# A graph-attention and expert layer: first pair of graphs on raw x and raw W with rank-one corrections

## The chip, the cores and the metric

One core of one Trainium2 chip. The metric is device time in microseconds (us): the median of three runs, lower is better. A profile of one further execution shows what each engine did: PE (TensorE; its weight loads are listed apart as PEld), DVE (VectorE), ACT (ScalarE), POOL (GpSimd) and SP (which issues most transfers).

## The reference

x holds 128 graphs of 128 nodes with 1024 features each; adj holds one 0/1 matrix per graph. Cut to what matters:

```python
xn = layernorm(x)                               # mean and variance over the 1024 features
Wh = xn @ W                                     # W: 1024 x 1024, 16 heads of 64 columns
e = leaky_relu(Wh @ a1 + Wh @ a2, 0.2)          # one score per node and head
att = softmax(where(adj == 0, NEG_INF, e)) * adj
x = x + elu(att @ Wh)
xn = layernorm(x)
gates = softmax of the 2 largest of xn[:, 0] @ router.T, per graph
x = x + xn + sum over 8 experts of gates * (xn @ down.T) @ up
```

A score depends on its node alone, so a row of `att` is one number wherever adj is 1.

## The kernel before, in words

**Pairs.** The kernel works on pairs of graphs, q = 0 to 63. For each pair, `project(q)` multiplies a 256 x 1024 block of x with W by Winograd's variant of Strassen's scheme: seven products instead of eight, each of a 128 x 512 block with a 512 x 512 block. W's quarters are B11, B21, B22 and (in the slot of T1) W12; from them `combine` (L756) makes T3 = B22 - W12, T2 = T3 + B11, T1 = B22 - T2, NT4 = B21 - T2. On the side of x, `pair_sums` (L339 to L342, POOL) makes s1 to s4 from the transposed tiles `xt`. A product is 8 program matmuls in f32 (L383; 16 entries in the profile). Products 1 and 2 share the PSUM bank x, 6, 5 and 3 the bank y, 7 and 4 the bank z; there are two such PSUM buffers. `read` (L391, DVE) takes sums out of them: u2 after product 6, u4 after product 5, and the three blocks of `wh` later. Product 5 accumulates in the bank from which u2 is read.

**Layernorm without normalizing x.** W is centred (the mean of each column over the rows is taken off), so that x needs no mean subtraction, and 1/std (`RSTD`) is applied afterwards in `high` (L452, ACT) and `low` (L456, DVE), which split a result into two parts for the f32r matmuls of `attend` (L498). Scores come with the products: each block of W has four more columns, the centred W times a (260 columns instead of 256).

**The first pair.** All this has to be prepared while pair 0 is running; its centring of W is only done by `center_block` (L212, DVE) step by step. In the kernel before, pair 0 takes centred x (`center_x`, L186 to L196: means by PE, subtraction by DVE) times partly raw W; `correct_p1` (L771) mends p1, which the other products use. Column means of W come from `partial_means` (`fourths`, L180: four column tiles of PE of 32 columns at once), an ACT copy (L183) and `column_means` (L203). The score columns come from the transposed W: `score_rows` (L223), `center_rows` (L232 to L238), `turn_rows` (PE transposes, L247) and `score_columns` (L257 to L262, DVE). They are not ready for pair 0 itself: `score_of` multiplies pair 0's results with a (L273, POOL) and sums by head (L207, DVE).

**Order.** Nothing is scheduled by itself: every engine executes in the order in which the program records the instructions. `for q` (L804) fills eight lists, gaps[0] to gaps[7]; the tasks of gaps[i] are recorded just before the i-th product of the pair. `prepare` (L777) fills those of pair 0. Attention of pair q is done under the products of pair q + 1: `attention_weights` (L460) is in gaps[0] of pair q + 1, `attend` and `update` in gaps[1] and gaps[2], where `update` ends with L516 and L517 on DVE around an Exp on ACT (L515). Statistics of x are bn_stats and bn_aggr on DVE (`stats`, L312). The experts' tables (router, down) are centred once, during pair 1: `over_chunks` (L276) and `experts` (L286). A group of two pairs goes through the experts two pairs later.

**Transfers.** SP issues the loads in program order (from L117); adj_f goes through POOL's queue (L108). All x tiles, the transposed W's second half and, after the change, two more tiles share ten buffers with the tag "x".

## Time and profile before

| what | us |
| --- | --- |
| median of 3 runs | 1971.35 (1970.18 to 1971.63) |
| the profiled execution | 1970.7 |
| its span in the profile | 1968.8 |
| first product of pair 0 starts | 11.88 |
| score rows on PE (L223) start | 39.03 |
| first attention weights (L489, pair 0) | 69.45 |
| first product of pair 2 starts | 96.66 |

The span is the stretch in which the profile saw instructions; the execution's own time is 1.9 us longer. A line of the profile names the source line, the engine, the operation, the tile written and those read, with their shape. A wait is put down to whatever ended last before it, by semaphores. Idle time of an engine that is not the bottleneck costs nothing.

### The profile page before, as it was taken

To read this page: it belongs to the slowest core of one execution; us is meant where nothing else is said; L and a number is where in the kernel's file an instruction comes from. 1 tells how busy PE (TensorE), PEld (TensorE's weight loads), DVE (VectorE), ACT (ScalarE), POOL (GpSimd) and SP (SyncE) were. 2 spreads that over 40 slices of the span, in tenths; PEclk is the share of its full clock that TensorE was granted. 3 is DMA by queue.
4 is the path that set the end of the run, shared out by engine and by line. 5 is a ranking of instruction groups with operands and counts; after the bars stand their busy time and mean duration, and the time that the engine had idled before them with its cause. 6 is when DMAs were issued, how large, how long until landed. Compare 5 with 4: busy or idle time off the path is not lost.

```text
span 1968.8 us, 30168 instructions
## 1 busy us (share of the span) xinstructions
PE 1937.1 (98%) x11042; PEld 1575.5 (80%) x11042; DVE 1654.9 (84%) x3511; ACT 1080.4 (55%) x1032; POOL 833.1 (42%) x1123
## 2 busy tenths in 40 slices
PE   7899999999999999999999999999999999999997
PEld 4688888888888888888888888888888888888885
DVE  5888888888888888888898888898888898888886
ACT  1355555555655655555655655655655655655653
POOL 1443344543334543434544335544435544435530
PEclk9999999999999999999999999999999999999998
DMA  7265566565565565666565566565565565565552
GB/s 280 75 172 174 155 185 182 134 188 170 154 187 184 127 195 168 154 186 179 129 203 167 152 185 177 133 201 170 149 187 173 139 197 172 151 187 163 149 161 96
DMA packets 343671, 329.26 MB, mean 167 GB/s; under 512 B 274274, under 2 KB 276322, under 8 KB 342884
## 3 DMA queue, kind: packets, MB, share of 16 engines
q1 hardware_dynamic: 325940, 285.37, 49.6%
q0 software_dynamic: 17008, 40.91, 7.3%
q8 instruction: 88, 1.44, 0.3%
q10 hardware_dynamic: 576, 1.05, 0.1%
q14 instruction: 59, 0.48, 0.1%
HBM read 193.58 MB, written 67.63 MB: 133 GB/s over the span
## 4 chain that ended last, share of the span: by engine, by line
PE 91%; DVE 5%; DMA 2%; ACT 1%; issue 0%; POOL 0%; SPq 0%; DVEq 0%; POOLq 0%; ACTq 0%
PE pw L383 76%; PE ph L498 6%; PE pu L687 3%; PE pd L671 3%; DMA tt<-halves 1%; PE pb L634 1%; PE pl L578 1%; DVE stats L316 1%; DMA w_sb<-in_w 1%; ACT y_t L554 1%; DVE xn L516 1%; DVE hp L508 1%; DVE xn L517 1%; ACT halves L548 0%; PE pu L748 0%
## 5 line engine op out<-in xcount | busy, mean ns | idle before, releaser
L383 PE MATMUL pw<-w_sb,xt 128*128 128x260 f32 (+1 forms) x4096 | 953.0, 387 | 5.6 <-DVE parts L456 4.8
L383 PEld LDWEIGHTS pw<-w_sb,xt 128*128 128x128 f32 x4096 | 771.9, 191 | 153.5 <-issue 25.0
L383 PE MATMUL pw<-w_sb,s 128*128 128x260 f32 (+1 forms) x3072 | 712.9, 385 | 4.8 <-DVE w_sb L756 3.7
L383 PEld LDWEIGHTS pw<-w_sb,s 128*128 128x128 f32 x3072 | 579.6, 190 | 118.8 <-issue 24.8
L320 POOL TENSOR_SCALAR rstd<-mv 128x2 f32<-128x2 f32 x128 | 28.1, 219 | 868.0 <-DVE mv L317 862.7
L554 ACT COPY y_t<-tt 128x2048 uint16<-128x2048 uint16 x126 | 312.9, 2506 | 68.3 <-DMA tt<-halves 68.2
L316 DVE BATCH_NORM_STATS2 stats<-xn 128x6 f32<-128x512 f32 x512 | 323.8, 674 | 0.1
L652 POOL DMA_INDIRECT down<-table,at_down x248 | 251.4, 1014 | 163.8 <-DVE e L472 90.1
L548 ACT COPY halves<-xn 128x2048 uint16<-128x2048 uint16 x126 | 239.3, 1899 | 140.5 <-DVE xn L517 140.5
L452 ACT ACTIVATE parts<-wh,rstd 128x512 fp32r<-128x512 f32 x192 | 134.3, 716 | 224.0 <-DVE wh L391 223.8
L515 ACT ACTIVATE ex<-hp 128x1024 f32<-128x1024 f32 x128 | 135.3, 1057 | 182.6 <-DVE hp L508 182.6
L691 DVE SCALAR_TENSOR_TENSOR xn<-pu,rstd,xn 128x512 f32<-128x512 f32 x248 | 169.0, 744 | 21.8 <-PE pu L687 21.8
L508 DVE TENSOR_TENSOR hp<-ph,att 128x512 f32<-128x512 f32 x256 | 161.3, 671 | 10.0 <-PE ph L498 9.7
L498 PE MATMUL ph<-parts,adj_f 128*128 128x512 f32 x512 | 164.9, 442 | 4.5 <-DVE parts L456 3.7
L517 DVE SCALAR_TENSOR_TENSOR xn<-ex,xn 128x1024 f32<-128x1024 f32 x128 | 156.8, 1225 | 13.3
L391 DVE TENSOR_TENSOR wh<-pw,u 128x520 f32<-128x520 f32 (+1 forms) x128 | 89.2, 697 | 88.9 <-PE pw L383 85.5
L516 DVE SCALAR_TENSOR_TENSOR xn<-hp,xn 128x1024 f32<-128x1024 f32 x128 | 156.8, 1225 | 4.4
L570 ACT ACTIVATE xn<-xn,off,mul 128x1024 f32<-128x1024 f32 x128 | 151.4, 1233 | 1.5 <-POOL off L535 1.5
L456 DVE SCALAR_TENSOR_TENSOR parts<-wh,rstd,parts 128x512 fp32r<-128x512 f32 x192 | 139.4, 753 | 9.6 <-ACT parts L452 9.6
L498 PEld LDWEIGHTS ph<-parts,adj_f 128*128 128x128 f32 x512 | 96.5, 189 | 24.2 <-DVE parts L456 5.0
L391 DVE TENSOR_TENSOR wh<-pw,p 128x520 f32<-128x520 f32 (+1 forms) x64 | 44.7, 699 | 80.5 <-PE pw L383 80.5
L321 POOL TENSOR_TENSOR rstd<-rstd,half_pow 128x2 f32<-128x2 f32 x128 | 91.3, 713 | 10.7
(140 smaller groups left out, 1467.8 us busy)
## 6 DMA issues: line engine op xcount, KB each, us to landing
xt<-in_x_t SPq DMA_DIRECT2D x128, 512.0 KB, 5.2
xn<-in_x SPq DMA_DIRECT2D x128, 512.0 KB, 6.7
out_y<-xn SPq DMA_DIRECT2D x124, 512.0 KB, 3.8
adj_f<-in_adj_t POOLq DMA_DIRECT2D x32, 256.0 KB
adj_i<-in_adj SPq DMA_DIRECT2D x32, 256.0 KB, 2.6
w_sb<-in_w SPq DMA_DIRECT2D x4, 1040.0 KB, 7.3
down<-table,at_down POOLq DMA_INDIRECT x248, 3.7
wt_sb<-in_w_t SPq DMA_DIRECT2D x1, 2048.0 KB
```

Source lines behind the costliest of these rows:

```text
L316: nc.vector.bn_stats(st[:, h, :], X[i][:, h * HALF:(h + 1) * HALF])
L383: nc.tensor.matmul(dst[:, j, cols], lhs[:, k, :], w_sb[:, rhs, k, j, cols], start=(first and k == 0), stop=(k == KH - 1), skip_group_check ...
L456: nc.vector.scalar_tensor_tensor(in_two(PARTS[q][:, 1, b]), block, rstd, in_two(PARTS[q][:, 0, b].bitcast(F32)), op0=ALU.mult, op1=ALU.sub ...
L498: nc.tensor.matmul(PH[i][h], GRP[g]["adj_f"][:, t, :], PARTS[q][:, s, NH * (i % 2) + h], start=(s == 0), stop=(s == 1))
L508: nc.vector.tensor_tensor(hp[:, h * HALF:(h + 1) * HALF].rearrange("p (h f) -> p h f", f=F), ph.rearrange("p (h f) -> p h f", f=F), att[:, ...
L516: nc.vector.scalar_tensor_tensor(xt, hp, 0.0, xt, op0=ALU.max, op1=ALU.add)
L517: nc.vector.scalar_tensor_tensor(xt, ex, 1.0, xt, op0=ALU.min, op1=ALU.add)
L548: nc.scalar.copy(halves, X[i].bitcast(U16).rearrange("p (d s) -> p s d", s=2))
L554: nc.scalar.copy(y_of(i).bitcast(U16).rearrange("p k (n s) -> p s k n", s=2), TT.pop(i).rearrange("p (s k) n -> p s k n", s=2))
L570: nc.scalar.activation(X[i], X[i], AF.Identity, bias=GRP[g]["off"][:, t:t + 1], scale=GRP[g]["mul"][:, t:t + 1])
L652: nc.gpsimd.indirect_dma_start(out=st["down"][:, j * R:(j + 1) * R].rearrange("p r k -> p (r k)"), out_offset=None, in_=table, in_offset=b ...
L691: nc.vector.scalar_tensor_tensor(y[:, cols], pu[t], st["rstd"][:, t:t + 1], y[:, cols], op0=ALU.mult, op1=ALU.add)
```

## The change

In pair 0 x is no longer centred. Products 1 and 2 use raw x and raw B11 and B21, and `correct` (DVE, new L804) puts right their sum (c11, kept in SBUF) and p1 by adding the column means of W times minus the row sums of x; other products take centred or difference blocks, for which raw x is right. The transfers are put in another order and split. Twelve matmuls on a constant tile, whose result nobody reads, stand before the first product. The statistics of graphs 0 to 3 move from DVE to ACT, with small POOL steps (`sums_of`, `less`, `squares_of`). Pair 0's scores come from a PE product of xt with the score columns in column tiles (`first_scores`, in the middle of product 4, and `turn_scores`); score columns are placed by ACT (new L238) and combined by POOL (new L251 to L257). Sums over the experts' tables move from DVE to PE (`table_parts`). s3 of pair 0 gets its own tile, and within a product of pair 0 the two halves of the columns alternate. Line numbers of the kernel before hold elsewhere with a shift.

```diff
@@ -112,38 +111,48 @@
...
-    a_sum = work.tile([P, NH, 2, QC], F32, tag="ex", name="a_sum", bufs=1)
-    a_rows = work.tile([2, D], F32, tag="parts", name="a_rows", bufs=1)
-    nc.sync.dma_start(a_rows, a)
     a_cols = small.tile([P, 2, KC], F32, tag="a_cols", name="a_cols", bufs=1)
-    nc.sync.dma_start(a_cols, a_t)
-    load_xt(0)
+    nc.scalar.dma_start(a_cols, a_t)
+    xt = XT[0] = work.tile([P, 2, KC, P], F32, tag="xt", name="xt")
+    nc.sync.dma_start(xt[:, 0, 0:KH], x_t[0, :, 0:KH])
+    for k in range(0, KH, 2):
+        nc.sync.dma_start(w_sb[:, B11, k:k + 2], w[:, 0, k:k + 2])
+    nc.sync.dma_start(w_sb[:, B21], w[:, 1])
+    nc.sync.dma_start(xt[:, 0, KH:KC], x_t[0, :, KH:KC])
+    nc.sync.dma_start(xt[:, 1], x_t[1])
+    for i, b in ((2, B22), (3, T1)):
+        nc.sync.dma_start(w_sb[:, b], w[:, i])
+    load_x(0)
     wt_sb = work.tile([P, KH, D], F32, tag="y_t", name="wt_sb", bufs=1)
     wt_at = [wt_sb[:, c] for c in range(KH)]
     wt_at += [work.tile([P, D], F32, tag="x", name="wt", bufs=10) for _ in range(KH)]
-    for i, b in enumerate((B11, B21, B22, T1)):
-        if i == 2:
-            load_x(0)
-        nc.sync.dma_start(w_sb[:, b], w[:, i])
     nc.sync.dma_start(wt_sb, w_t[:, 0:KH])
     for c in range(KH, KC):
         nc.sync.dma_start(wt_at[c], w_t[:, c])
+    first_s3 = work.tile([P, 2, KH, P], F32, tag="x", name="first_s3", bufs=10)[:, 0]
+    scratch = work.tile([P, D], F32, tag="x", name="scratch", bufs=10)
     router_sb = const.tile([P, KC, E], F32, name="router_sb")
     down_sb = work.tile([P, G * TOP, R, KC], F32, tag="down", name="down_sb", bufs=1)
-    load_adj(0)
...
+    mean_of, sum_of = (work.tile([P, P], F32, tag="dn", name=n) for n in ("mean_of", "sum_of"))
+    nc.vector.memset(mean_of, 1.0 / D)
+    nc.vector.memset(sum_of, 1.0 / 32)
+    idle = ps_m.tile([P, P], F32, tag="pm", name="idle")
+    for _ in range(12):
+        nc.tensor.matmul(idle, mean_of, mean_of, start=True, stop=True)
...
-    mean_of, sum_of = (work.tile([P, P], F32, tag="dn", name=n) for n in ("mean_of", "sum_of"))
-    nc.vector.memset(mean_of, 1.0 / D)
-    nc.vector.memset(sum_of, 1.0 / 32)
+    fold = small.tile([P, H], F32, tag="fold", name="fold", bufs=1)
+    nc.vector.tensor_reduce(fold, ident.rearrange("p (t h) -> p h t", t=KH)[:, 0:H], AX.X, ALU.add)
@@ -163,37 +172,21 @@
...
-    def spread_a():
...
+    def fourths(*parts):
+        sizes = [rows[0].free_size() for rows in parts]
+        pc = ps_m.tile([P, HALF], F32, tag="pm", name="pc")[:, 0:sum(sizes)]
+        at = 0
+        for rows, n in zip(parts, sizes):
+            for u in range(2):
+                for c in range(KH):
+                    nc.tensor.matmul(pc[c * 32:(c + 1) * 32, at:at + n], mean_of[:, 0:32],
+                                     rows[u * KH + c], start=(u == 0), stop=(u == 1),
+                                     tile_position=(0, c * 32))
+            at += n
+        part = work.tile([P, HALF], F32, tag="hp", name="part")[:, 0:at]
...
-    def center_x():
@@ -240,54 +230,62 @@
...
+            for half in range(2):
+                nc.scalar.copy(
+                    a_two[:, u * KH:(u + 1) * KH, half * HPH:(half + 1) * HPH].rearrange(
+                        "p k (t f) -> p k t f", f=2),
+                    pt.rearrange("p k (t r) -> p k t r", t=KH)[:, :, :, 2 * half:2 * half + 2])
+    def score_columns():
+        def own(u, h):
+            return a_two[:, u * KH:(u + 1) * KH, h * HPH:(h + 1) * HPH].rearrange(
+                "p k (j c) -> p k j c", j=2)
         of = {b: w_sb[:, b, :, :, SCORES] for b in range(7)}
-        for h, u, dst in ((0, 0, of[B11]), (0, 1, of[B21]), (1, 1, of[B22]), (1, 0, b12)):
...
-    def score_of(b):
...
-    def over_chunks():
...
+        b11, b21, b22, b12 = own(0, 0), own(1, 0), own(1, 1), own(0, 1)
+        nc.gpsimd.tensor_copy(of[B11], b11)
+        nc.gpsimd.tensor_tensor(of[T3], b22, b12, ALU.subtract)
+        nc.gpsimd.tensor_tensor(of[T2], of[T3], b11, ALU.add)
+        nc.gpsimd.tensor_copy(of[B21], b21)
+        nc.gpsimd.tensor_tensor(of[T1], b22, of[T2], ALU.subtract)
+        nc.gpsimd.tensor_copy(of[B22], b22)
+        nc.gpsimd.tensor_tensor(of[NT4], b21, of[T2], ALU.subtract)
+    def first_scores():
+        ps = ps_m.tile([P, HALF], F32, tag="pm", name="ps")[:, 0:2 * P]
+        for u in range(2):
+            for c in range(KH):
+                k = u * KH + c
+                nc.tensor.matmul(ps[c * 32:(c + 1) * 32], a_two[:, k], xt[:, :, k],
+                                 start=(u == 0), stop=(u == 1), tile_position=(0, c * 32))
+        part = work.tile([P, 2, P], F32, tag="hp", name="part")
+        nc.scalar.copy(part, ps.rearrange("p (t n) -> p t n", t=2))
+        return part
+    def turn_scores(part):
+        ps = ps_m.tile([P, HALF], F32, tag="pm", name="ps")
+        for t in range(2):
+            nc.tensor.matmul(ps[:, t * H:(t + 1) * H], part[:, t], fold, start=True, stop=True)
+        SC[0] = small.tile([P, 2, H], F32, tag="sc0", name="sc0", bufs=1)
+        nc.scalar.copy(SC[0], ps[:, 0:2 * H].rearrange("p (t h) -> p t h", t=2))
+    def table_parts():
+        return fourths([router_sb[:, k] for k in range(KC)],
+                       [down_sb.rearrange("p e r k -> p k (e r)")[:, k] for k in range(KC)])
...
-        nc.tensor.matmul(pr[:, 0:E + ER], mean_of, GRP["sums"], start=True, stop=True)
+        nc.tensor.matmul(pr[:, 0:E + ER], sum_of, part, start=True, stop=True)
@@ -329,6 +327,36 @@
...
+    def sums_of(i):
+        q, t = divmod(i, 2)
+        if t == 0:
+            MV[q] = small.tile([P, 2, 6], F32, tag="row_sums", name="row_sums", bufs=2)
+        mv = MV[q][:, t]
+        for h in range(NH):
+            nc.scalar.activation(scratch[:, h * HALF:(h + 1) * HALF],
+                                 X[i][:, h * HALF:(h + 1) * HALF], AF.Identity,
+                                 accum_out=mv[:, h:h + 1])
+        nc.gpsimd.tensor_tensor(mv[:, 2:3], mv[:, 0:1], mv[:, 1:2], ALU.add)
+        nc.gpsimd.tensor_scalar(mv[:, 3:4], mv[:, 2:3], -1.0 / D, None, op0=ALU.mult)
+    def less():
+        got = small.tile([P, 3], F32, tag="less", name="less", bufs=1)
+        nc.gpsimd.tensor_scalar(got, MV[0][:, 0, 0:3], -1.0, None, op0=ALU.mult)
+        return got
+    def squares_of(q):
+        for t in range(2):
+            mv = MV[q][:, t]
+            nc.scalar.activation(scratch, X[2 * q + t], AF.Square, bias=mv[:, 3:4],
+                                 accum_out=mv[:, 4:5])
+        RSTD[q] = small.tile([P, 2], F32, tag="rstd", name="rstd")
+        nc.gpsimd.tensor_scalar(RSTD[q], MV.pop(q)[:, :, 4], 1.0 / D, EPS, op0=ALU.mult,
+                                op1=ALU.add)
+        nc.gpsimd.tensor_tensor(RSTD[q], RSTD[q], half_pow.to_broadcast([P, 2]), ALU.pow)
@@ -338,9 +366,10 @@
...
-        nc.gpsimd.tensor_tensor(a21, a11, a21, ALU.subtract)
+        s3 = a21 if q else first_s3
+        nc.gpsimd.tensor_tensor(s3, a11, a21, ALU.subtract)
@@ -377,12 +407,16 @@
...
-        def product(dst, first, lhs, rhs):
-            for j in range(2):
-                for k in range(KH):
-                    nc.tensor.matmul(dst[:, j, cols], lhs[:, k, :], w_sb[:, rhs, k, j, cols],
-                                     start=(first and k == 0), stop=(k == KH - 1),
-                                     skip_group_check=not first)
+        def product(dst, first, lhs, rhs, half_way=None):
+            order = [(j, k) for j in range(2) for k in range(KH)]
+            if q == 0:
+                order.sort(key=lambda at: at[1])
+            for at, (j, k) in enumerate(order):
+                if half_way and at == KH:
+                    half_way()
+                nc.tensor.matmul(dst[:, j, cols], lhs[:, k, :], w_sb[:, rhs, k, j, cols],
+                                 start=(first and k == 0), stop=(k == KH - 1),
+                                 skip_group_check=not first)
...
-            product(*to("z"), a22, NT4)
+            product(*to("z"), a22, NT4, None if q else keep("scores", first_scores)[0])
...
+        sc = SC.pop(q)
+        for dst, raw in (((blocks[:, 1:], WH[q][:, :, :, SCORES]), (blocks[:, 0], sc)) if q
+                         else ((e, sc),)):
@@ -758,45 +794,40 @@
...
-    def first_half():
...
-    def correct_p1(less):
...
+        bank = WH[0, 0]
+        WH[0, 0] = work.tile([P, 2, QC], F32, tag="hp", name="c11")
+        nc.scalar.copy(WH[0, 0], bank[:, :, MAIN])
+    def correct(less):
+        for c, by in ((WH[0, 0], less[:, 2:3]), (WH["p1"][:, :, MAIN], less[:, 0:1])):
+            nc.vector.scalar_tensor_tensor(c, w_mean[0], by, c, op0=ALU.mult, op1=ALU.add)
...
-        gaps[0] += [(place_a,), (spread_a,), (center_x,), (pair_sums, 0)]
-        gaps[1] += [keep("part 0", partial_means, 0)]
-        gaps[2] += [keep("", column_means, "part 0"), (keep_c11,),
-                    (combine, T3, B22, T1, ALU.subtract), (first_stats, 0),
-                    keep("less", first_half), (first_stats, 1), (high, 0, 0)]
-        gaps[3] += [keep("part 1", partial_means, 1), keep("", column_means, "part 1"),
-                    (center_block, 0, B11), keep("", correct_p1, "less"),
-                    (combine, T2, T3, B11, ALU.add)]
-        gaps[4] += [keep("rows", score_rows), (center_block, 1, B22),
-                    (combine, T1, B22, T2, ALU.subtract), (center_block, 0, B21),
-                    keep("turned", center_rows, "rows")]
-        gaps[5] += [keep("cols", turn_rows, "turned"), (combine, NT4, B21, T2, ALU.subtract),
-                    (load_experts,)]
-        gaps[6] += [keep("", score_columns, "cols")]
+        gaps[0] += [(place_a,), (pair_sums, 0)]
+        gaps[1] += [keep("part 0", partial_means, 0), keep("", column_means, "part 0"),
+                    (center_block, 0, B11)]
+        gaps[2] += [(keep_c11,), keep("part 1", partial_means, 1),
+                    (combine, T3, B22, T1, ALU.subtract)]
+        gaps[3] += [keep("", column_means, "part 1"), (combine, T2, T3, B11, ALU.add),
+                    (sums_of, 0), keep("less", less), keep("", correct, "less"),
+                    (center_block, 1, B22),
+                    (combine, T1, B22, T2, ALU.subtract), (sums_of, 1), (squares_of, 0),
+                    (load_adj, 0), (high, 0, 0)]
+        gaps[4] += [(center_block, 0, B21), (combine, NT4, B21, T2, ALU.subtract), (low, 0, 0)]
+        gaps[5] += [keep("rows", score_rows), (load_experts,), keep("turned", center_rows, "rows")]
+        gaps[6] += [keep("", turn_rows, "turned"), (score_columns,)]
+        gaps[7] += [keep("", turn_scores, "scores")]
@@ -834,7 +865,7 @@
...
-            gaps[4 if q else 6].append((pair_sums, q + 1))
+            gaps[4 if q else 5].append((pair_sums, q + 1))
...
-            gaps[3].insert(0, (low, q, 0))
+            if q:
+                gaps[3].insert(0, (low, q, 0))
...
         if q == 0:
-            gaps[7] += [(score_of, 0), (score_of, 3), (score_of, 1), (score_of, 2)]
+            gaps[7] += [(sums_of, 2), (sums_of, 3)]
         if q == 1:
-            gaps[2][2:2] = [(first_stats, 2), (first_stats, 3)]
-            gaps[5].append((over_chunks,))
-            gaps[7].append((experts,))
+            gaps[0].append((squares_of, 1))
+            gaps[5].append(keep("tables", table_parts))
+            gaps[7].append(keep("", experts, "tables"))
```

## The prediction

> **What bounds the kernel now.** I read the page's busy shares first, then its chain of waits, then busy time by windows, and last PE's own waits and its timeline over the first 97 us.
>
> ```profile
> PE 1937.1 (98%) x11042; PEld 1575.5 (80%) x11042; DVE 1654.9 (84%) x3511; ACT 1080.4 (55%) x1032; POOL 833.1 (42%) x1123
> PE 91%; DVE 5%; DMA 2%; ACT 1%; issue 0%; POOL 0%; SPq 0%; DVEq 0%; POOLq 0%; ACTq 0%
> ```
>
> PE is idle for only 1968.8 - 1937.1 = 31.7 us in all. The windows say where.
>
> ```profile
> 0.00:30.00 30.00, 24.88 (x104) 14.34 (x104) 11.97 (x31) 5.29 (x9) 7.42 (x13) 1.00 0.94 372
> 30.00:60.00 30.00, 24.84 (x120) 17.97 (x121) 23.27 (x30) 3.27 (x5) 6.73 (x9) 0.94 0.35 119
> 60.00:96.66 36.66, 27.55 (x109) 22.08 (x108) 29.75 (x54) 16.47 (x15) 13.66 (x19) 0.91 0.27 75
> 240.00:300.00 60.00, 60.00 (x347) 49.26 (x347) 51.32 (x115) 34.52 (x34) 27.08 (x37) 1.00 0.59 167
> ```
>
> Columns: length, then busy time of PE, PEld, DVE, ACT and POOL, granted clock, DMA share, GB/s. Up to 96.66 us, where pair 2's first product starts, PE idles 5.12 + 5.16 + 9.11 = 19.4 us. Deep in the loop it never idles. So pairs 0 and 1 can lose time to waits, and a microsecond saved before pair 2 arrives whole at the end unless something new stalls PE.
>
> ```profile
> PE pw L383 <- DVE parts L456: 4.8, 1, 4.8
> PE pw L383 <- DVE w_sb L756: 3.7, 2, 2.0
> PE ph L498 <- DVE parts L456: 3.2, 2, 1.8
> PE pa L170 <- DMA a_rows<-in_a: 2.5, 1, 2.5
> PE pc L180 <- DMA xt<-in_x_t: 1.2, 1, 1.2
> ```
>
> DVE is the usual releaser: it prepares W, and in pair 1 it is late with the attention work. Some products are also slow:
>
> ```profile
> 11.88 6.30 PE L383 MATMUL pw<-w_sb,xt 128*128 128x256 f32 x16 [0.78 <-DVE xt L195]
> 24.38 3.62 PE L383 MATMUL pw<-w_sb,xt 128*128 128x256 f32 x16
> 33.72 5.38 PE L383 MATMUL pw<-w_sb,s 128*128 128x256 f32 x16 [1.98 <-DVE w_sb L756]
> 82.90 6.68 PE L383 MATMUL pw<-w_sb,xt 128*128 128x260 f32 x16 [4.85 <-DVE parts L456]
> ```
>
> The same 16 passes take 3.62 us when PE has been running and 5.38 to 6.68 after a wait: 2.7 + 1.8 + 3.0 = 7.5 us more. (A program matmul in f32 is two passes.)
>
> **What the Trainium skill says.** "TensorE: Matmul & The Clock Gate", Part 1 (the HAM clock gate): PE runs at half clock until one free-running window of 3413 ns has been busy. The three slow products agree, and the granted clock reads 0.55 and 0.59 over 34 to 38 us; the stall of 1.73 us before the product at 44.41 cost no slow product, so short stalls can pass free. Part 3 there (packing): 32-column tiles run side by side. Agrees: 16 tiled 512-wide passes (L180) take 1.93 us, two untiled ones (L203) 1.02. "SBUF — State Buffer", section "SBUF: two separate sides": a DVE operation with two SBUF inputs and a POOL operation lock each other out. Agrees: while POOL forms pair sums, a 32-element L262 takes 1.26 us against 0.16 for a 16-element copy (L257, a PSUM source), and two L456 take 2.87 instead of 1.5.
>
> **The change, part by part.** I lay the new order of each engine out with the old durations. PE's pitch from product to product is 3.45 us (50.03 to 53.49), less than a row's 3.62 because ends overlap.
>
> *Transfers.* Windows of 1 us show DMA at about 430 GB/s from 5 to 20 us, in issue order. T1's block, 6.64 MB into the queue, landed at 19.9 us, when 7.06 MB had moved: a lag of 0.4 MB. `a_rows`, `a_cols` and xt led the SP queue; now half an xt tile leads, at 0.74 instead of 1.58 us, so the curve comes 0.8 us sooner; adj_f (0.26 MB) leaves the front and x moves behind W. Same curve: half of B11 5.5 us, all of it 6.7, B21 9.2, rest of xt 11.1, T1 at 5.3 MB 16.1, x at 17.3 and 18.5, last of W transposed about 28.6. a_cols goes to the ACT queue (8 KB); behind it stands only the table load, needed at 11. adj_i goes on SP behind pair 1's x (12.9 MB, about 34.5 us; needed near 38), adj_f on POOL behind the first rstd (27.5; 0.8 us to issue; needed by ph at 49.65), where pair 1's pair sums wait behind it for s1 until 33.2 anyway.
>
> *Idle matmuls.* Not in the trace: 24 passes of 128 columns from 1.05 us. Half of a 256-wide pass gives 0.11 us warm (24: 2.7 us); the cold weight load (0.34 at most, L383) gives 8.1. I take 6.4, so product 1 starts at 7.5 us, warm; ends kept: 6.7 (data) and 9.2. Removed with `center_x`, `spread_a`: 3.75 + 1.93 + 1.22 us of PE, mostly in waits, and 2.42 us of DVE ahead of product 1, which started at 11.88 and ended at 18.1. At 3.5 us it now ends at 11.0.
>
> *Pair 0.* Partial means 1.9 (to 12.9). ACT copies (0.59); w_mean starts after 0.7 us of waiting, ends 14.5. Product 2 to 18.0, second means to 19.85. DVE: center B11 (2.28) 14.75 to 17.0, T3 (2.29) to 19.3, so product 7 does not wait: 19.85 to 23.3; w_mean 1 to 24.2; T2 done at 21.6, product 6 to 27.65. ACT: c11 copy, part copy, two half-row sums of x to 22.0. No row shows ACTIVATE with an accumulator: from 0.58 (copy of 512) to 1.0; I take 0.7, and 1.2 per square (1.06 for L515, to 1.5). Three small POOL steps (0.2 to 0.25 like L320) to 22.8; the two corrections (0.74 like L771) to 24.3, just ahead of w_mean 1. Then DVE alone sets the pace: center B22, T1, and `u2`, which stands behind both: 24.4 + 2.28 + 2.28 + 0.7 = 29.7. Product 5 accumulates in the bank that u2 reads: PE waits 2.1 us, and product 5 starts at 29.75, against 44.4. Behind u2, B21, NT4, `low`, u4 run to 36.2 (POOL's next pair sums, from 33.2, add about 0.5) while PE does product 5 and the score rows (3.8, to 37.0). Product 3 to 40.45, transposes to 41.6, half of product 4 to 43.3, scores of the pair (16 tiled 256-wide passes, half of 1.93: 1.0) to 44.3, rest to 46.0, fold 0.2: pair 1 starts at 46.2 instead of about 57.0. Squares and rstd on ACT and POOL end near 27.5 and are needed at 34.3: hidden. POOL's seven score operations on 32 elements are unseen: 0.2 (L353) to 0.7 (L321) each, I take 0.3; they lie under product 4, and even 0.7 ends before product 6 of pair 1 needs T2's column.
>
> *Pair 1.* Gone from DVE: the 8 copies and 4 differences of score columns (5.3 us), 4 reductions L207 (2.7), two rows' statistics (2.9), sums over experts (1.5). ACT gets four sums and two squares ahead of `ex`; behind these wait Exp, the p1 copy and ex, and DVE waits for them. wh lands 46.85, two lows to 48.35, five small steps to 49.3; ACT is through the sums at 50.55, Exp 50.8; att at 51.9, 5.7 us after pair 1's start, against 12.6 before (69.64 - 57.0). The x update then: hp 53.2, squares on ACT until 53.3, p1 53.9, ex 55.0, L517 to 56.2, u2 56.9. PE: product 1 to 49.65, ph, product 6 to 54.3, ph, product 2 to 58.9, product 5 to 62.35. `low` of pair 1's first block ends at 62.95 on DVE: product 7 waits 0.6 us, against 4.85 plus a cold product. To 66.4; table sums on PE (32 tiled passes, as eight groups of four at 0.12 to 0.25: 1.0 to 2.0, take 1.6) to 68.0; product 3 and product 4 to 74.9, pr 0.3: pair 2 at 75.3, against 96.66. Beyond pair 2 each engine's instructions stand in the old order, with the same kinds of waits apart from a few DMA semaphores.
>
> **Sum.** 75.3 - 96.66 = -21.4 us on the profiled 1970.7 (span 1968.8): 1949.3; the median of 1971.35 gives 1950.0. Counted from PE's side: 96.66 - 19.4 idle - 7.5 cold - 6.9 dropped work + 2.8 added (scores 1.0, fold 0.2, tables 1.6) + 6.45 idle matmuls + 4.45 idle (1.05 + 0.7 + 2.1 + 0.6) = 76.6, 1.3 more than the chain; handovers of 0.05 to 0.1 us, some ten on the path, are in no duration either. I add 1.0: 1951.0.
>
> **Rivals.**
> A. Pair 1 stays late. Against my 0.6 us wait: sums at 1.0 and squares at 1.5 push Exp, ex and low by 1.8 us, the stall at product 5 of pair 0 or product 7 sends PE cold once or twice (1.8 to 3.0 each as in the trace). 1951 + 1.8 + 4.2 = 1957. For it: every long wait shown was followed by a slow product; against: one of 1.73 was not.
> B. Transfers rule: if T1 still lands at 19.9, T3 ends at 22.2 and product 7 starts 2.4 us later: 1953.4. Against it: x's 1.05 MB (2.4 us at 430 GB/s) now stand behind T1.
> C. Half is given back: pairs 2 and 3 were already tight (PE waited 1.06 us in 96.66 to 150), and a DVE backlog carried over takes 10 us: 1961.
> D. Slower: two more tiles (first_s3, scratch) pass through the ten x buffers, so later x and output transfers pair up differently. If that puts one eviction (L391, 0.70 us) per pair on PE's path, 62 pairs cost 43 us: 1994. It decides from 21 / 62 = 0.34 us per pair upwards. Against it: DMA share 0.59 in the loop, no PE wait there, an unchanged instruction order.
>
> **How the numbers follow.** Forecast 0.60 (1948 to 1954), A 0.20, B 0.09, C 0.05, D 0.04, and no change 0.02, were the end set by something that the chain hides. Predicted 1951.0. The low end is the data start of the idle phase (-0.8), no cold product, no added 1.0 and 1 us for cheaper table sums and stalls: 1947.5; the high end takes A with two cold products at 3.0 each (1951 + 1.8 + 6.0): 1959. What can be told from no change is 0.2%, 3.9 us: faster 0.94 (forecast, A, B, C), same 0.02, slower 0.04.
>
> **What would show it.** Right: product 1 starts at 6.7 to 9.2 us and takes near 3.6; product 5 of pair 0 waits about 2 us for DVE u; pair 1 starts near 46, pair 2 near 75; no idle slice later. Wrong: 5 to 7 us for product 7 of pair 1, PE waiting for w_sb behind DMA, ACT between DVE p and att for over 2 us, or windows of the loop with PE below 60 of 60.

## The result, and the profile after

The changed kernel takes 1948.7 us, the median of four runs (1947.16 to 1949.08); the kernel before, run beside it, takes 1970.76 us (1970.04 to 1971.63). The ratio is 0.9886, with a 95% interval from 0.9869 to 0.9904. The prediction was 1951.0 us, with a range from 1947.5 to 1959.0: the time lies inside, 2.3 us below the predicted one. The profiled execution took 1949.08 us, its span 1947.3 us, against 1970.7 and 1968.8 before.

The page's busy line and the engines' shares of the chain of waits, in the order in which the prediction showed them:

```profile
PE 1931.7 (99%) x11096; PEld 1574.6 (81%) x11096; DVE 1638.3 (84%) x3477; ACT 1089.6 (56%) x1060; POOL 832.7 (43%) x1135
PE 95%; DVE 2%; ACT 1%; DMA 0%; issue 0%; POOL 0%; POOLq 0%; DVEq 0%; ACTq 0%
```

PE is idle for 1947.3 - 1931.7 = 15.6 us instead of 31.7, and the chain that ended last runs through PE for 95% of the span instead of 91%; DVE's share of it fell from 5% to 2% and that of DMA from 2% to 0%. The windows of the changed kernel show where (length, then busy time of PE, PEld, DVE, ACT and POOL, granted clock, DMA share, GB/s):

```profile
0.00:30.00 30.00, 26.39 (x128) 19.73 (x129) 16.05 (x27) 9.30 (x18) 8.42 (x18) 1.00 0.94 377
30.00:60.00 30.00, 30.00 (x169) 22.78 (x168) 23.54 (x37) 14.25 (x30) 11.36 (x21) 1.00 0.54 181
60.00:74.15 14.15, 14.15 (x92) 11.57 (x92) 9.01 (x17) 10.55 (x10) 7.77 (x13) 1.00 0.27 52
240.00:300.00 60.00, 60.00 (x346) 49.23 (x347) 51.28 (x110) 34.44 (x34) 26.82 (x36) 1.00 0.59 167
```

Pair 2 starts at 74.15 us instead of 96.66. Up to there PE idles 3.6 us instead of 19.4, all of it in the first 30 us, and the granted clock reads 1.00 throughout, where it was 0.94 and 0.91. In the loop PE is busy for 60 of 60 us, as before. PE's waits by releaser, in the changed kernel, name the three that are left on this stretch (total us, times, longest):

```profile
PE pw L417 <- DVE u L425: 1.9, 1, 1.9
...
PE idle L149 <- DVE mean_of L144: 1.1, 1, 1.1
...
PE w_mean L196 <- ACT part L188: 0.7, 1, 0.7
```

The waits for `a_rows`, for xt, for `parts` and for w_sb are gone from this stretch. In PE's timeline of the changed kernel (start, duration, then line, operation, tiles, and in brackets the idle time before and its releaser):

```profile
1.05 5.49 PE L149 MATMUL idle<-mean_of 128*128 128x128 f32 x24 [1.05 <-DVE mean_of L144]
6.33 4.00 PE L417 MATMUL pw<-w_sb,xt 128*128 128x256 f32 x16
...
29.18 3.72 PE L417 MATMUL pw<-w_sb,s 128*128 128x256 f32 x16 [1.85 <-DVE u L425]
...
62.02 3.67 PE L417 MATMUL pw<-w_sb,xt 128*128 128x260 f32 x16
65.62 0.31 PE L183 MATMUL pc<-router_sb,mean_of 128*32 128x8 f32 x16
65.77 1.11 PE L183 MATMUL pc<-down_sb,mean_of 128*32 128x128 f32 x16
...
74.15 3.67 PE L417 MATMUL pw<-w_sb,xt 128*128 128x260 f32 x16
```

Up to pair 2 no product takes 5.4 to 6.7 us any more. Product 7 of pair 1 (62.02) follows without a gap. In the kernel before it waited 4.85 us and then ran cold, that is at about half the full clock: over 82.9 to 89.5 us the granted clock reads 0.55 there. The shift then holds: the ACT copy of p1 (L405 before, L439 after), which follows each pair's product 1, starts 22.51 us earlier in pair 2, 22.60 earlier in pair 31 and 22.70 earlier in pair 63. For pair 2, in ACT's timeline, before and after:

```profile
100.55 0.58 ACT L405 COPY p<-pw 128x520 f32<-128x520 f32 x1
78.04 0.57 ACT L439 COPY p<-pw 128x520 f32<-128x520 f32 x1
```

The span gained only 21.5, because the last stage gave 1.2 us back: its 16 up-projection matmuls, with the same instructions in the same order, take 8.85 us before the change (first line) and 10.05 after it (second line).

```profile
1955.81 8.85 PE L748 MATMUL pu<-w_sb,dn_all 128*128 128x512 f32 x16 [1.03 <-issue]
1933.11 10.05 PE L784 MATMUL pu<-w_sb,dn_all 128*128 128x512 f32 x16 [1.03 <-issue]
```

### The profile page after: what moved, and what is told of

It reads as the page before. It is cut to its first block, busy times and chain, and to the rows that moved or that the text cites. A ratio compares the mean times of both kernels' runs of the same rounds, so it can differ in the third digit from the quotient of the medians.

```text
span 1947.3 us, 30291 instructions
## 1 busy us (share of the span) xinstructions
PE 1931.7 (99%) x11096; PEld 1574.6 (81%) x11096; DVE 1638.3 (84%) x3477; ACT 1089.6 (56%) x1060; POOL 832.7 (43%) x1135
## 4 chain that ended last, share of the span: by engine, by line
PE 95%; DVE 2%; ACT 1%; DMA 0%; issue 0%; POOL 0%; POOLq 0%; DVEq 0%; ACTq 0%
PE pw L417 80%; PE ph L534 6%; PE pu L723 3%; PE pd L707 3%; PE pb L670 1%; PE pl L614 1%; PE pu L784 1%; DMA tt<-halves 0%; DVE xn L553 0%; DVE hp L544 0%; DVE xn L552 0%; PE idle L149 0%; DVE stats L314 0%; ACT xn L606 0%; DVE parts L490 0%
## 5 line engine op out<-in xcount | busy, mean ns | idle before, releaser
L314 DVE BATCH_NORM_STATS2 stats<-xn 128x6 f32<-128x512 f32 x504 | 318.8, 674 | 0.1
L319 POOL TENSOR_TENSOR rstd<-rstd,half_pow 128x2 f32<-128x2 f32 x126 | 89.7, 712 | 10.5
```

The costliest lines, as they stand in the source:

```text
L314: nc.vector.bn_stats(st[:, h, :], X[i][:, h * HALF:(h + 1) * HALF])
```

## The experiments

The runs of one kernel spread over 0.5 to 5 us, as much as many effects looked for here. The traces are sharper. So each experiment is read first by the start of pair 2's p copy (78.04 us in the changed kernel): what delays PE up to the steady loop is in it, and nothing of the last stage. (It stands on ACT behind an Exp that waits for DVE. In two runs, statistics on DVE and old scores, this makes it 0.3 us later than PE itself: there pair 2's first product starts only 2.51 and 2.17 us later than in the changed kernel.) The idle matmuls themselves last 4.37 to 5.49 us in the ten profiles with 24 of them, so the last column takes the start of product 1 off. It still contains the length of product 1, 3.62 to 5.88 us.

| run | time, us: median (range) | product 1 starts | pair 2's p copy | distance |
| --- | --- | --- | --- | --- |
| changed kernel | 1948.7 (1947.16 to 1949.08) | 6.33 | 78.04 | 71.71 |
| no idle matmuls | 1948.45 (1948.29 to 1951.91) | 5.64 | 80.69 | 75.05 |
| twice as many | 1950.96 (1950.04 to 1951.76) | 9.21 | 80.55 | 71.34 |
| old transfers | 1950.7 (1949.6 to 1954.47) | 8.52 | 79.92 | 71.40 |
| x centred first | 1952.21 (1951.83 to 1953.47) | 8.89 | 81.79 | 72.90 |
| statistics on DVE | 1949.89 (1948.95 to 1951.2) | 5.55 | 80.85 | 75.30 |
| old scores | 1951.37 (1948.82 to 1952.31) | 6.18 | 80.47 | 74.29 |
| both of these | 1955.67 (1953.62 to 1957.03) | 5.47 | 85.83 | 80.36 |
| wait filled | 1945.99 (1944.95 to 1946.27) | 5.62 | 75.29 | 69.67 |
| last stage covered, first try | 1948.74 (1948.44 to 1948.94) | 5.79 | 77.41 | 71.62 |
| last stage covered | 1946.75 (1945.36 to 1947.83) | 5.31 | 77.22 | 71.91 |
| wait filled, last stage covered | 1943.74 (1943.46 to 1945.12) | 6.33 | 75.90 | 69.57 |

The kernel before took 1969.91 to 1971.13 us (medians) beside these runs.

### The idle matmuls: none, and twice as many

```diff
-    idle = ps_m.tile([P, P], F32, tag="pm", name="idle")
-    for _ in range(12):
-        nc.tensor.matmul(idle, mean_of, mean_of, start=True, stop=True)
```

> The changed kernel without the twelve idle matmuls. Theory (sum of parts: each part is worth what it takes off PE's path, and the shift then runs to the end): product 1 starts when its data are there, 5.5 to 6 us instead of 6.33, and runs cold, 6.3 us instead of 4.0, so it ends near 12 instead of 10.3; pair 2's first product 1.5 to 2.2 us later (75.7 to 76.3 against 74.15), time about 1950.5. Rival 'the clock is the gain' (the idle matmuls keep PE warm through all of pair 0, and without them the small waits of pair 0 keep it cold): two to four more slow products, pair 2 at 80 or later, time 1955 or more. Rival 'the idle phase is pure cost': product 1 ends earlier than 10.3 and the time falls.

PE's timeline without them:

```profile
5.64 5.88 PE L414 MATMUL pw<-w_sb,xt 128*128 128x256 f32 x16 [5.64 <-DMA w_sb<-in_w]
...
30.33 5.41 PE L414 MATMUL pw<-w_sb,s 128*128 128x256 f32 x16 [1.85 <-DVE u L422]
```

Product 1 starts when the first W lands, 0.7 us earlier, and takes 5.88 us instead of 4.00: what follows it is 1.18 us later. That is what the idle matmuls buy, as long as they don't reach past 5.64 us by much. The second line is a surprise: the wait before product 5 is the same 1.85 us as in the changed kernel, but product 5 takes 5.41 us here and 3.72 there. This profile is of the slowest of its four runs (1951.91); the other three lie at 1948.29 to 1948.53, level with the changed kernel. So the 1.18 us is shown in the trace, and the times don't resolve it.

With 24 program matmuls instead of 12:

```diff
-    for _ in range(12):
+    for _ in range(24):
```

> Twenty-four idle matmuls instead of twelve, so product 1 is started late on purpose. Theory (every delay ahead of product 1 reaches the end whole, since only DVE's T3 follows close behind): 24 more passes at 0.11 (half of a warm 256-wide pass) to 0.23 us (5.49 us for 24), so product 1 starts 2.7 to 5.5 us later, but is fully warm (3.6 instead of 4.0 us); pair 2 is 2 to 5 us later, by the same amount as product 1's end, and so is the time (1951 to 1954). Rival 'T3 and the transfers set the pace of pair 0': product 7 is at 19.3 anyway bound by W's last block, and pair 2 moves by less than half of product 1's delay.

They last 8.32 us, product 1 starts at 9.21, and pair 2's p copy is 2.51 us later (80.55). The distance from product 1 hardly changes (71.34). So up to pair 2 nothing hides a later start of product 1: it is the head of the chain. An earlier start is not worth as much: in the five runs in which product 1 starts at 5.31 to 5.79 us (statistics on DVE, both parts, wait filled, and the two of the last stage alone), product 7 waits 0.25 to 0.52 us for T3, which DVE can't make before the last block of W lands.

### The order of the transfers, and raw x

In the next run xt, B11, B21, x, B22 and T1 are loaded in the old order and unsplit; raw x stays.

```diff
-    nc.sync.dma_start(xt[:, 0, 0:KH], x_t[0, :, 0:KH])
...
-    for i, b in ((2, B22), (3, T1)):
+    for t in range(2):
+        nc.sync.dma_start(xt[:, t], x_t[t])
+    for i, b in enumerate((B11, B21, B22, T1)):
+        if i == 2:
+            load_x(0)
```

> The changed kernel with the loads in the order of the kernel before: both xt tiles whole, B11, B21, x, then B22 and T1. Theory: product 1 waits for B11 (2.1 MB into the queue: about 7.7 us instead of 6.3), and T1 lands near 19 instead of 16.9, so T3 is done near 21.5 and product 7 starts there instead of at 19.3; pair 2 is 1.5 to 3 us later, time 1950 to 1952. Rival 'transfers are hidden anyway': product 7 and pair 2 stay within 0.5 us. Rival 'transfers are most of the gain': 6 us or more.

PE's timeline of this run:

```profile
8.52 3.69 PE L414 MATMUL pw<-w_sb,xt 128*128 128x256 f32 x16 [1.98 <-DMA w_sb<-in_w]
...
21.14 3.72 PE L414 MATMUL pw<-w_sb,first_s 128*128 128x256 f32 x16
```

The new order is worth 1.88 us (79.92 against 78.04), and all of it comes at product 1, which waits 1.98 us for B11: it starts 2.19 us later, and its row is 0.31 us shorter. T1's block lands at 18.48 us, but product 7 (second line) does not wait for what is made of it. Rival B of the prediction had put the cost of the transfers there.

The next run keeps raw W but takes the mean off x before product 1, with `center_x` of the kernel before and xt's tiles first in the queue; only p1 is corrected.

```diff
...
-        gaps[0] += [(place_a,), (pair_sums, 0)]
+        gaps[0] += [(place_a,), (center_x,), (pair_sums, 0)]
...
-        for c, by in ((WH[0, 0], less[:, 2:3]), (WH["p1"][:, :, MAIN], less[:, 0:1])):
+        for c, by in ((WH["p1"][:, :, MAIN], less[:, 0:1]),):
```

> The first pair's x is centred before product 1 again, as in the kernel before (its tiles first in the queue, means by TensorE, subtraction on VectorE); the raw W with its one correction stays. Theory (the raw x takes the mean and the subtraction off the path to product 1): product 1 starts at 9.7 to 10.5 us against 6.33, and pair 2's p copy is 3.2 to 4.2 us later, 81.2 to 82.2; time 1951.5 to 1953. Rival (the order of the transfers alone decides, as in the run with the old order): product 1's end and pair 2's p copy no more than 2 us later.

Its PE timeline:

```profile
7.41 0.70 PE L195 MATMUL px<-part,sum_of 128*128 128x256 f32 x2 [0.49 <-ACT part L187]
8.89 3.72 PE L429 MATMUL pw<-w_sb,xt 128*128 128x256 f32 x16 [0.78 <-DVE xt L199]
...
31.43 5.41 PE L429 MATMUL pw<-w_sb,s 128*128 128x256 f32 x16 [1.86 <-DVE u L437]
```

Product 1 starts at 8.89 us, earlier than the 9.7 to 10.5 expected, and its row is 0.28 us shorter (3.72 against 4.00). Pair 2's p copy is 3.75 us later, inside the expected 3.2 to 4.2, but 1.7 of that is the cold product 5, which had not been expected: that the number fits is chance. Raw x and its place in the queue are therefore worth 2.3 us at the end of product 1 (12.54 against 10.27 for what follows it), between the rival's 2 and the theory's 3.2. It acts on the same start of product 1 as the order of the transfers does; how far the two add wasn't tried.

### DVE's relief: statistics, scores, and both

Statistics of graphs 2 and 3 go back to DVE, in pair 1:

```diff
-            gaps[7] += [(sums_of, 2), (sums_of, 3)]
...
-            gaps[0].append((squares_of, 1))
+            gaps[2][2:2] = [(first_stats, 2), (first_stats, 3)]
```

> Pair 1's row statistics back on DVE (bn_stats and bn_aggr, ahead of the second graph's update, as in the kernel before) instead of ACT. Theory: DVE gets 2.9 us more ahead of low of pair 1's first block, ACT 4.9 us less ahead of Exp and ex, which gives about 1 us back; that block's low ends near 63.5 instead of 61.6, and product 7 of pair 1 (62.0) waits 1.5 us for it; pair 2 1.5 us later, time about 1950; up to 3 us more if the wait sends PE cold. Rival 'only the scores mattered, the statistics were beside the path': no wait at product 7, pair 2 within 0.3 us.

Its PE timeline (product 5 of pair 0, product 7 of pair 1):

```profile
28.35 5.41 PE L417 MATMUL pw<-w_sb,s 128*128 128x256 f32 x16 [1.85 <-DVE u L425]
...
64.42 3.77 PE L417 MATMUL pw<-w_sb,xt 128*128 128x260 f32 x16 [1.58 <-DVE parts L490]
```

The wait before product 7 is back, at 1.58 us. Pair 2's p copy is 2.81 us later. Of this, 1.58 + 1.69 for the cold product 5, less 0.78 for the earlier product 1, makes 2.5, which is what PE lost: its first product of pair 2 starts at 76.66 instead of 74.15. The other 0.3 is on ACT alone. What the statistics themselves cost is the wait of 1.6 us.

Next, pair 0's scores as in the kernel before: products with a on POOL, sums by head on DVE. The PE scores are left out.

```diff
...
-            product(*to("z"), a22, NT4, None if q else keep("scores", first_scores)[0])
+            product(*to("z"), a22, NT4, None)
...
-        gaps[4] += [(center_block, 0, B21), (combine, NT4, B21, T2, ALU.subtract), (low, 0, 0)]
+        gaps[4] += [(spread_a,), (center_block, 0, B21), (combine, NT4, B21, T2, ALU.subtract), (low, 0, 0)]
...
-        gaps[7] += [keep("", turn_scores, "scores")]
...
+            gaps[7] += [(score_of, 0), (score_of, 3), (score_of, 1), (score_of, 2)]
```

> The first pair's scores are made as in the kernel before (a copied to a_rows on ACT's queue, spread_a in the wait before product 5, products on POOL, sums on VectorE); the rest is the changed kernel. Theory (the scores by column tiles are what gets the first e of pair 0 out early and keeps VectorE free): TensorE loses about 1.3 us of work (first_scores and the fold) so pair 1's product 1 starts up to 1.3 us earlier, but e comes some 5.5 us later than wh1 allows, VectorE has 2.7 us more to do, the low half of pair 1's first block comes 3.5 to 5.5 us later, and product 7 of pair 1 waits 3 to 5 us and then runs at the half clock (5.4 us instead of 3.8). Pair 2's p copy at 81 to 85 against 78.0, time 1951 to 1955. Rival (the scores were hidden anyway): pair 2's p copy within 0.5 us of 78.0 or up to 1.3 us before it.

PE's timeline of pair 1 in this run:

```profile
54.92 3.74 PE L443 MATMUL pw<-w_sb,xt 128*128 128x260 f32 x16 [1.70 <-ACT p L465]
...
64.08 3.77 PE L443 MATMUL pw<-w_sb,xt 128*128 128x260 f32 x16 [1.91 <-DVE parts L516]
```

On DVE `e` starts 6.54 us after the last block of wh (43.94 to 50.48) instead of 1.93 us (45.88 to 47.81); in between DVE also stands idle for 0.82 and 0.54 us, waiting for POOL's products. Two waits come back, 3.6 us together, one of them for ACT's copy of p1. The p copy of pair 2 comes at 80.47, just short of the 81 expected: neither wait made a product cold.

Each part alone brings a wait that leaves PE warm. Both together:

> The first pair's scores as in the kernel before (products on POOL, sums on VectorE) and its row statistics on VectorE as well; transfers, raw x and idle passes stay. Theory (the load on VectorE decides pair 1's wait, and the two parts add): the waits of pair 1 sum to 5 us or more (3.6 with the old scores alone, 1.6 with the old statistics alone), one product at the half clock, and pair 2's p copy at 82.5 to 85.5 against 78.0, 80.5 and 80.9. Rival (one covers the other, since both only fill the same wait): no later than 81.5.

```profile
58.17 3.75 PE L443 MATMUL pw<-w_sb,s 128*128 128x260 f32 x16 [1.59 <-DVE u L451]
66.70 6.77 PE L443 MATMUL pw<-w_sb,xt 128*128 128x260 f32 x16 [4.79 <-DVE parts L516]
```

This is PE's timeline of pair 1 again, and the second line is the old stall: 4.79 us of waiting and a product of 6.77, against 4.85 and 6.68 in the kernel before. Pair 2's p copy is at 85.83, beyond the expected 82.5 to 85.5, and 7.79 us later than in the changed kernel, where the two parts alone cost 2.43 and 2.81 (1.69 of the latter for a cold product 5, ahead of which PE has `spread_a` to do here). So the old statistics and the old scores together are what made pair 1 late, through DVE's `low`. How much of it is DVE's load and how much the longer way to `e` over POOL is not separated. The cost is more than additive: behind the longer wait the product is cold (granted clock 0.55), which takes 3.0 us more. The median of 1955.67 is 7.0 us above that of the changed kernel.

Not every part of the change was taken back alone. What follows product 1 comes 7.84 us earlier than before (10.27 against 18.11), pair 1 about 11 us earlier (46.04 against about 57.0), pair 2 22.51 us earlier. The runs above bear on the first of these steps and on most of the last. The new order of pair 0 behind product 1, the score columns on ACT and POOL and the table sums on PE have no run of their own: their share is read from the timelines and not shown by an experiment.

### The wait that is left, and the last stage

The 1.85 us before product 5 stand because u2 waits on DVE behind B22's centring and T1's combination. PE has the score rows to do just behind product 5, and half of them need nothing that is late. `low` of block 0 moves behind u4 in the same run:

```diff
...
-        gaps[4] += [(center_block, 0, B21), (combine, NT4, B21, T2, ALU.subtract), (low, 0, 0)]
-        gaps[5] += [keep("rows", score_rows), (load_experts,), keep("turned", center_rows, "rows")]
-        gaps[6] += [keep("", turn_rows, "turned"), (score_columns,)]
+        gaps[4] += [keep("half", score_rows, 0, None), (center_block, 0, B21),
+                    (combine, NT4, B21, T2, ALU.subtract)]
+        gaps[5] += [keep("rows", score_rows, 1, "half"), (load_experts,), keep("turned", center_rows, "rows")]
+        gaps[6] += [keep("", turn_rows, "turned"), (score_columns,), (low, 0, 0)]
```

> The first half of the score rows of the first pair is put into TensorE's wait before product 5, where the changed kernel leaves 1.85 us idle, and the low half of block 0 is taken behind u4 on VectorE. Theory (that wait is the last one before pair 2 that costs anything): product 5 starts as before without an idle TensorE ahead of it and is always at the full clock, the score rows no longer stand behind product 4a, and pair 2's p copy comes about 1.0 to 1.8 us earlier, 76.2 to 77.0; time 1946.5 to 1947.8. Rival (the wait goes to the next product, since u4 on VectorE is late by as much): a wait before product 3 or 4 of 0.8 us or more and a gain under 0.8 us.

PE's timeline of this run:

```profile
26.42 1.92 PE L214 MATMUL rows<-wt_sb,a_two 128*32 128x512 f32 x16
28.34 3.72 PE L418 MATMUL pw<-w_sb,s 128*128 128x256 f32 x16
31.99 1.92 PE L214 MATMUL rows<-wt,a_two 128*32 128x512 f32 x16
33.85 3.72 PE L418 MATMUL pw<-w_sb,s 128*128 128x256 f32 x16
```

There is no idle time ahead of any of the four. From product 1 to pair 2's p copy it takes 69.67 us instead of 71.71: 2.04 less, slightly more than the 1.0 to 1.8 expected. Of this, 0.13 is a shorter product 1 (3.62 us, not 4.00) less a wait of 0.25 us before product 7. No later product waits for u4. The time is 1945.99 us, with all four runs below the fastest of the changed kernel.

In the last stage PE waits for DVE and ACT, and some of its work runs at the half clock: in the changed kernel the last 16 passes of the down product take 3.79 us at a granted clock of 0.50, the same shape some 7 us earlier 2.05 at 1.00. The first try puts products of a constant tile in these waits, written to the spare half of `pd_all`:

```diff
+    def keep_warm(g, n):
+        for _ in range(n):
+            nc.tensor.matmul(GRP[g]["junk"], ident, ident, start=True, stop=True)
...
+        keep_warm(i // G, 7 if i % 2 else 2)
...
+        keep_warm(g, 5)
         pg = ps_m.tile([P, HALF], F32, tag="pm", name="pg")
...
     def up_dense(g):
         st = GRP[g]
+        keep_warm(g, 7)
```

> The changed kernel with products of a constant tile (results read by nobody) in TensorE's waits of the last stage: 9 before the transposes, 5 before pg, 7 before the last up products. Theory (the last stage runs at the half clock because TensorE waits there for VectorE and ACT): the last 16 up products take about 7.1 us instead of 10.05, the last down products about 2.1 instead of 3.8, and the time is 3 to 4.5 us below the changed kernel, 1944 to 1946. Rival (the last stage is set by VectorE and ACT, or the clock does not come up in time): 1947.5 to 1950, no shorter up products.

The end of PE's timeline in this run:

```profile
1926.83 2.05 PE L760 MATMUL pd_all<-y_t,w_sb 128*128 128x128 f32 x16
...
1932.66 3.36 PE L595 MATMUL pd_all<-ident 128*128 128x128 f32 x14 [0.98 <-DVE dn_all L781]
1935.81 7.13 PE L792 MATMUL pu<-w_sb,dn_all 128*128 128x512 f32 x16
```

The down products take 2.05 us instead of 3.79, the up products 7.13 instead of 10.05, as expected, and the time stays: 1948.74. The middle line shows why. The last constant products wait for `dn_all`, since DVE reads the tile that they write; then they run at the half clock (0.50) for 3.36 us, on the path. The up products start 21.21 us after the first down product instead of 18.30, and the 2.9 us that they save are gone. With a PSUM tile of their own, and 10 of them before pg and 4 after it (shown against the first try):

```diff
...
-            nc.tensor.matmul(GRP[g]["junk"], ident, ident, start=True, stop=True)
+        junk = ps_m.tile([P, P], F32, tag="pm", name="junk")
+        for _ in range(n):
+            nc.tensor.matmul(junk, ident, ident, start=True, stop=True)
```

> The last stage of the changed kernel is covered as in the run before (constant products in TensorE's waits), but the products go to a PSUM tile of their own, so that they do not wait for dn_all, 10 of them before pg and 4 before the up products. Theory (the cover works, and the run before gave the gain back because its last 7 products waited 0.98 us for dn_all and then ran 3.36 us at the half clock on the path): the 16 up products start where they did in the changed kernel, about 20.2 us after the first down product (1933.1 - 1914.8 = 18.3, plus or minus 0.5), run in about 7.1 us instead of 10.05, and the time is 2 to 3.5 us below the changed kernel. Rival (the cover itself costs what it brings, or the store that ends last sets the end): under 0.7 us of gain.

```profile
1930.96 0.35 PE L776 MATMUL pg<-ident,chosen_rows 4*128 4x4 f32 x2 [0.27 <-DVE chosen_rows L772]
1931.24 1.16 PE L596 MATMUL junk<-ident 128*128 128x128 f32 x8
1932.34 7.11 PE L792 MATMUL pu<-w_sb,dn_all 128*128 128x512 f32 x16
```

In PE's timeline the up products start 18.16 us after the first down product (18.30 in the changed kernel; the 20.2 in the expectation is a slip for the difference that stands behind it) and take 7.11 us. The faster down products alone bring next to nothing, since pg still waits for DVE's `chosen_rows` (first line). The median is 1946.75 us, 1.95 below the changed kernel, just short of the 2 to 3.5 expected; the two ranges overlap (1945.36 to 1947.83 against 1947.16 to 1949.08), so that the gain rests on the trace more than on the times. Both edits together:

> The changed kernel with the first half of the score rows in the wait before product 5 and the covered last stage together. Theory (the two waits lie at the two ends of one TensorE chain and add): pair 2's p copy at 75.3 to 76.2, the up products about 7.1 us, the time 1943 to 1944.5, some 4.5 to 5.5 us below the changed kernel. Rival (the gains overlap or the loop takes one of them back): 1945 to 1947.

1943.74 us (1943.46 to 1945.12), a ratio of 0.9862 to the kernel before, from 0.9846 to 0.9879: 5.0 us below the changed kernel, and every run below its fastest. Within the spread the gains add (2.7 and 1.95 alone), and this is the fastest of the kernels here. In its profile, of the slowest of its four runs, the last down products take 3.68 us again, at a granted clock of 0.53, and the up products start 19.48 us after the first down product: the cover doesn't hold every time.

## Why the prediction was right, point by point

**Product 1.** Predicted at 7.5 us, measured at 6.33. The term that was mis-sized is the idle phase: 6.4 us taken, 5.3 measured (1.05 to 6.33). The bounds, 2.7 all warm and 8.1 all cold, hold. The prediction's "warm" was not quite right either: the row takes 4.00 us, not 3.62, so the end was 10.27 against 11.0.

**Waits of pair 0.** w_mean's 0.7 us came exactly. T1 was put at 16.1 us and landed at 16.9, so DVE waited 0.54 us for it; product 7 still had no wait (19.32, predicted 19.85). The wait for u2 was put at 2.1 us with product 5 at 29.75; it is 1.85 us, with product 5 at 29.18, behind the very operations named (B22's centring and T1's combination, 2.29 us each, then u).

**Pair 1 starts** at 46.04 (predicted 46.2). Of the 1.17 us gained at product 1, 0.16 are left. Most of the difference: product 1's slow row took 0.44 (3.94 us to its successor instead of 3.5), product 3 and the two halves of product 4 took 0.37 together (3.56 and twice 1.83 instead of 3.45 and twice 1.7), the fold 0.16 (0.36 instead of 0.2). `low` of pair 0 took 1.76 us instead of about 0.75 while POOL made pair sums. Here the Trainium skill ("SBUF — State Buffer", section "SBUF: two separate sides") is borne out: VectorE and GpSimd lock each other out where VectorE has two SBUF inputs. L224, with two inputs of one element, took 1.05 us beside the last of these sums (the same operation, L234 before, 0.16 while POOL was idle); L225 after them, with one input, took 0.15. One reading of the prediction belongs elsewhere: the two L456 of 2.87 us lay beside POOL's products with a (L273) and not beside its pair sums.

**Attention of pair 0.** The step from pair 1's start to the end of `att` was put at 5.7 us instead of 12.6; it is 5.0 (51.02 - 46.04). The ACT sums, which no row of before showed, were taken at 0.7 us from a range of 0.58 to 1.0. ACT's timeline of the changed kernel shows them in two parts:

```profile
47.23 0.61 ACT L337 ACTIVATE scratch<-xn 128x512 f32<-128x512 f32 x1
47.75 0.19 ACT L337 ACTIVATION_READ_ACCUMULATOR scratch<-xn 128x1 f32 x1
47.84 0.61 ACT L337 ACTIVATE scratch<-xn 128x512 f32<-128x512 f32 x1
```

One sum every 0.61 us: the fetch of the accumulator is an instruction of its own, and overlaps for the most part. The squares, taken at 1.2, come every 1.33 us.

**Product 7 of pair 1** was to wait 0.6 us. It doesn't: `low` ends at 61.59, and PE arrives at 62.02. The slack is 0.43 us. The old scores take it away and leave a wait of 1.91 us, the old statistics one of 1.58, both one of 4.79.

**Tables and pair 2.** The table sums were taken at 1.6 us and cost 1.2 (65.62 to 66.80). Pair 2 starts at 74.15 instead of 75.3: 0.6 for the wait, 0.4 for the tables and the 0.16 of pair 0. So the gain up to there is 22.51 us (predicted 21.4). The 1.0 us added for handovers was not needed: the chain without it was already 1.15 too long, and the count from PE's side was too high by the idle phase (1.2), the idle time (4.45 taken, 3.60 measured) and the table sums.

**The end.** That nothing later takes anything back held for 62 pairs, but not for the last stage, of which the prediction said nothing: 22.70 us there became 21.5 in the span. The up products ran 1.2 us longer at a lower granted clock (0.71 against 0.80). This can't be put down to the change: in eight other profiles of kernels that leave this stage as it is, the same 16 take 8.55 to 10.14 us. Why the clock comes up sooner or later there is not shown.

**The sum.** That the chain's 21.4 us are the 21.5 of the span is in part luck: the start brought 1.1 us more than the chain said, and the last stage, which it left out, took 1.2 back. The low end of the range is also added wrongly: the terms named for it (0.8, 1.0 and 1) lead to 1948.2, not to 1947.5.

**Rivals.** A (pair 1 late and cold) is not what happened, but the run with both old parts on DVE is just that case. B fell: T1 does not decide even under the old order. But nothing is to spare: in the changed kernel product 7 starts 2.43 us after DVE begins T3, and in the five runs in which it waits for T3 it starts 2.44 us after. C and D fell: PE is busy for 60 of 60 us in the window of the loop, and the shift grows by 0.2 us from pair 2 to pair 63.

## What to carry to other kernels

Before a steady loop that one engine bounds, look at each microsecond of the start as if it were on the end: here what PE gained up to pair 2 was still there 60 pairs later, and a wait was filled with that engine's own work that was due soon anyway. Price an added load on a helper engine by the slack of what is queued behind it: each of two parts alone brought 1.6 to 3.6 us of waits there, both brought 6.4 and a cold product. If an engine is kept busy with dummy work, give that work its own buffer and let it wait for nothing; the first try here made it wait for the very result that it was to bridge.

## What the runs showed of the hardware that had not been expected

The same wait can cost the clock or not. In eight profiles PE waits 1.85 or 1.86 us before product 5, in the same order of instructions around it; five times the product then takes 3.72 us, three times 5.41. "TensorE: Matmul & The Clock Gate", Part 1 of the Trainium skill, says that the window over which activity is judged is free-running; these rows fit that, since nothing in the programs sets the phase, but no run here measures the phase. The three slow ones are slow by the clock: over each of them it reads 0.68. So a wait of this length has a price of nothing or 1.7 us. Elsewhere, products behind waits of 1.58, 1.70 and 1.91 us took 3.74 to 3.77 us, and one behind 1.98 us, in the kernel before, 5.38. This can make single times of one kernel differ, and it makes the positions in the trace the better measure.

The 24 idle passes vary too: 4.37 to 5.49 us in ten profiles. Here the profile's clock is no help. It reads 1.00 from 5.6 to 11.5 us of the run without idle matmuls, where product 1 takes 5.88 us, and from 12 to 18 us of the kernel before, where it takes 6.30. So that first slow product, which the prediction counts with the two others, is known as slow by its length alone.
